# Two pixels instead of four in a row of the corner table of a deformable convolution

## The chip, the cores and the metric

The kernel runs on one core of one Trainium2 chip, in fp32. The metric is the device time of one execution in microseconds (us); the runs shown are three executions of the kernel before.

## The reference

The input x has four images of 128 channels and 64 x 64 pixels. Two layers are applied to it.

Layer 0 normalizes x in groups of channels and adds a deformable 3 x 3 convolution of the result. An ordinary convolution gives, for every pixel and each of the nine taps, an offset (dy, dx) and a mask. The tap samples the normalized image at a fractional position by bilinear interpolation between four corners; what is outside the image counts as zero. The 9 x 128 samples of a pixel, times their masks, are multiplied by the convolution's weight.

```
y0, x0 = floor(py), floor(px);  wy, wx = py - y0, px - x0
v = v00*(1-wy)*(1-wx) + v01*(1-wy)*wx + v10*wy*(1-wx) + v11*wy*wx
out = einsum('bckhw,ock->bohw', v * mask, weight) + bias
```

Layer 1 sees the 4096 pixels of an image as 4096 tokens of 128 numbers, normalizes them, and applies attention and a feed-forward net:

```
qkv = ring products of cos(heads + theta)      # 16 heads of 8 numbers; q = k = v
ctx = softmax(q q^T / sqrt(8)) q               # over all 4096 tokens of the image
x1  = LN(x + ctx W);  out = LN(x1 + FFN(x1))
```

A mixture of eight experts, of which each token takes the best two, follows with another normalization and a residual. The output has the shape of x.

## The kernel before, in words

**Stages.** Each image is a batch b. `prepare(b)` does layer 0 and makes the keys, queries and values: `group_norm`, `corner_table`, `offsets`, then `deform`, which runs over 8 chunks of 512 pixels and starts `convolved` and `features` for each chunk. The attention of batch b runs over head groups (4 groups of 4 heads), chunks of 512 queries and 32 blocks of 128 keys. A step computes the scores of one block (`scores`, TensorE at L1143, the exponential on ScalarE at L1152) and adds their product with the values (`context`, L1160). For most pairs of neighbouring query chunks, exponentials computed once are transposed, written to DRAM (`etd`, L1045), fetched again (`et`, L1079) and used at L1099. `finish` does the rest of layer 1 for a chunk.

**Order.** The program of TensorE, VectorE, SyncE and GpSimd is written out in one order by a planner, `Beside`. It holds estimates of durations and puts pieces of `prepare`, `finish` and others between the attention steps: each piece says by `need(...)` what it costs on TensorE and VectorE, and `beside.later(...)` puts off a DMA until what it sends should be ready. Nothing of that changes at run time. SyncE (SP) issues nearly all DMAs in this order: what stands behind a DMA in its queue waits until that one has been issued, and one that waits for data holds up all that follow. ScalarE (ACT) issues the constants' loads at the start, and then some table writes. GpSimd (POOL) issues the gathers.

Batch 0 has nothing to run beside it: it is prepared alone until its first chunk is done, and then the first head group's attention takes keys as they come. `prepare(b + 1)` runs beside the attention of batch b.

**The table.** The image with a border is 67 x 67 = 4489 positions (`TW` = 67). In DRAM each position has a row of `4 * C` = 512 numbers (2 KB): the pixels at its four corners. There are two tables, used by even and odd batches. A gather (L573) fetches 128 rows, one for each of 128 output pixels, for one tap:

```
nc.gpsimd.indirect_dma_start(
    out=v[:, k, :], out_offset=None, in_=tab,
    in_offset=bass.IndirectOffsetOnAxis(ap=idx[:, j, kk : kk + 1], axis=0),
)
```

VectorE multiplies three such fetches by the twelve weights `wt` (L587), adds the four corners in two steps (L589, L590) and transposes the sums (L597).

**Filling the table.** `borders` writes zeros to two rows and two columns on each side: two DMAs of 67 columns x 2 rows (L303) and two of 63 rows x 2 columns (L304) a table. For table 0 they stand near the head of ACT's queue, ahead of `wom_sb` (L310, the weights of the offsets), `bom_sb` (L314) and the other constants. For table 1 they stand in SP's queue at the start of `prepare(1)`, just behind the four loads of the image (L764). The tile framework makes each pixel write wait for the borders of its table, and each gather for all writes before it.

`corner_table` takes four chunks of 1024 pixels. A chunk is normalized (L454), transposed on TensorE (L462), copied to a tile `tok` (L465, three buffers, which `deform` uses too) and written to the table (L474). A pixel is a corner of four positions, so `put` writes each chunk four times (k = 0 to 3), for odd and even image rows apart (`par`): 8 DMAs of 256 KB a chunk, 32 a batch, each in pieces of 512 bytes. In batch 0 ACT issues the odd k.

`offsets` computes in two halves: the convolution on TensorE (L505), a bias on VectorE (L512), a transpose (L517, L520), then on VectorE the floor, the index `idx` (L549) and the weights `wt` (L557), with an exponential for the mask on ACT (L527).

Of the kernel before, what the change touches and what calls it, by code (L numbers as in the profile page):

```python
# [9 lines left out]
F32 = mybir.dt.float32  # L10
# [3 lines left out]
ALU = mybir.AluOpType  # L14
# [9 lines left out]
C = 128  # L24
HH = 64
WW = 64
# [11 lines left out]
TW = WW + 3  # L38
# [157 lines left out]
def need(pe=0.0, dve=0.0, lat=0.0, hold=False, after=0.0):  # L196

    return pe, dve, lat, hold, after  # L200


def ve(n, ops=1):

    return ops * (0.17 + n / 960.0)
# [6 lines left out]
def tr(n):  # L212

    return 0.13 + 0.115 * n
# [3 lines left out]
def kernel(  # L218
# [22 lines left out]
    nc = tc.nc  # L241
# [7 lines left out]
    dram = ctx.enter_context(tc.tile_pool(name="table", bufs=1, space=DRAM))  # L249
# [14 lines left out]
    def misc(name):  # L264
        if alone:
            return ps_s.tile([P, 2, 512], F32, tag="sc", name=name)[:, 0, :]
        return ps_m.tile([P, 512], F32, tag="misc", name=name)
# [25 lines left out]


    NTAB = 2
    tabs = [dram.tile([TW * TW, 4 * C], F32, name=f"tab{i}") for i in range(NTAB)]
    def borders(tab, queue):
        zero = work.tile([P, 4, 4, P], F32, tag="st", name="zero", bufs=NST)
        zero = zero.rearrange("p r h x -> p r (h x)")[:TW, :2]
        nc.gpsimd.memset(zero, 0.0)  # L300
        tv = tab.rearrange("(y x) c -> y x c", x=TW)
        for s in (0, TW - 2):
            queue.dma_start(out=tv[s : s + 2].rearrange("y x c -> x y c"), in_=zero)  # L303
            queue.dma_start(out=tv[2 : TW - 2, s : s + 2, :], in_=zero[: TW - 4])  # L304

    borders(tabs[0], nc.scalar)

    wom_sb = cpool.tile([P, KK, 32], F32, name="wom_sb")
# [87 lines left out]
    for i in range(NFX):  # L396
        t = big.tile([P, 4, QR], F32, name=f"fx{i}")
        nc.gpsimd.memset(t, 0.0)
        h = t[:, :, : HEADS * QW].rearrange("p j (h d) -> p j h d", d=QW)
# [47 lines left out]
    def corner_table(b, xc, mg, rs, tab):  # L447


        tv = tab.rearrange("(y x) (k c) -> y x k c", x=TW, c=C)  # L450
        for ch in range(NBLK // 8):
            yield need(dve=ve(1024), lat=0.3)
            part = xc[:, 1024 * ch : 1024 * (ch + 1)]
            nc.vector.tensor_scalar(part, part, mg, rs, ALU.subtract, ALU.mult)  # L454
            tok = work.tile([P, 3, 4 * C], F32, tag="v", name=f"tok{b}_{ch}", bufs=NV)
            tok = tok.rearrange("p k (q c) -> p (k q) c", c=C)[:, :8]
            for i in range(0, 8, 4):
                yield need(pe=tr(4), dve=ve(512), lat=FREE)
                pt = misc(f"tok_ps{b}_{ch}_{i}")
                for n in range(4):  # L460
                    j = 8 * ch + i + n
                    nc.tensor.transpose(  # L462
                        pt[:, C * n : C * (n + 1)], xc[:, P * j : P * (j + 1)], ident
                    )
                nc.vector.tensor_copy(  # L465
                    tok[:, i : i + 4, :], pt.rearrange("p (i c) -> p i c", c=C)
                )
            def put(ch=ch, tok=tok):
                for par in range(2):
                    for k in range(4):  # L470
                        y0 = 16 * ch + par + 2 - k // 2
                        x0 = 2 - k % 2
                        queue = nc.scalar if b == 0 and k % 2 else nc.sync
                        queue.dma_start(  # L474
                            out=tv[y0 : y0 + 15 : 2, x0 : x0 + WW, k].rearrange("y x c -> x y c"),
                            in_=tok[WW * par : WW * (par + 1)],
                        )

            beside.later(beside.dve, put)

    def offsets(b, xn, idx, wt):

        xn3 = xn.rearrange("p (h w) -> p h w", w=WW)
        HB = NBLK // 2
        for half in range(2):
            blk = slice(HB * half, HB * (half + 1))

            def temp(name, n):
                return work.tile([P, HB, n], F32, tag="p2", name=f"{name}{b}_{half}", bufs=NP2)

            for n, k in enumerate((4, 0, 1, 2, 3, 5, 6, 7, 8)):
                for top in range(0, 8, 4):
                    last = n == KK - 1 and top == 4
                    yield need(pe=MM256, dve=ve(512) if last else 0.0, lat=0.2 if last else FREE, hold=not last)
                    if n == 0 and top == 0:
                        po = misc(f"om_ps{b}_{half}")
                        p3 = po.rearrange("p (h w) -> p h w", w=WW)
                    dy, dx = k // 3 - 1, k % 3 - 1  # L500
                    for c in range(4):
                        r0 = 32 * half + 8 * c
                        ra, rb_ = max(r0 + top, -dy), min(r0 + top + 4, HH - dy)
                        ca, cb = max(0, -dx), min(WW, WW - dx)
                        nc.tensor.matmul(  # L505
                            p3[32 * c : 32 * (c + 1), ra - r0 : rb_ - r0, ca:cb],
                            lhsT=wom_sb[:, k, :],
                            rhs=xn3[:, ra + dy : rb_ + dy, ca + dx : cb + dx],
                            start=(n == 0 and top == 0), stop=last,
                        )  # L510
            oc = work.tile([P, 512], F32, tag="p2", name=f"oc{b}_{half}", bufs=NP2)
            nc.vector.tensor_scalar(oc, po, bom_sb, None, ALU.add)  # L512
            yield need(pe=tr(4), dve=ve(432), lat=0.2)
            om = temp("om", 27)
            pt = misc(f"oc_ps{b}_{half}")
            for i in range(4):
                nc.tensor.transpose(  # L517
                    pt[:, P * i : P * (i + 1)], oc[:, P * i : P * (i + 1)], ident
                )
            nc.vector.tensor_copy(  # L520
                om.rearrange("p (c i) k -> p i c k", i=4),
                pt.rearrange("p (i c k) -> p i c k", c=4, k=32)[:, :, :, :27],
            )

            yield need(dve=ve(288, 2))
            mk = temp("mk", KK)
            nc.scalar.activation(mk, om[:, :, 18:27], AF.Exp, scale=-1.0)  # L527
            p = om[:, :, 0:18]
            nc.vector.tensor_tensor(p, p, grid_sb[:, blk, :], ALU.add)
            nc.vector.tensor_scalar(p, p, LO, HI, ALU.max, ALU.min)  # L530
            yield need(dve=ve(288, 3))
            fl, up, ix = temp("fl", 18), temp("up", 18), temp("ix", KK)
            nc.vector.tensor_scalar(fl, p, ROUND, None, ALU.add)
            nc.vector.tensor_scalar(fl, fl, ROUND, None, ALU.subtract)
            nc.vector.tensor_tensor(up, fl, p, ALU.is_gt)
            yield need(dve=ve(288, 2))
            nc.vector.tensor_tensor(fl, fl, up, ALU.subtract)
            nc.vector.tensor_tensor(p, p, fl, ALU.subtract)
            yield need(dve=ve(144, 3) + 0.6)

            def of_axis(t, a):
                return t.rearrange("p j (k a) -> p j k a", a=2)[:, :, :, a]

            nc.vector.tensor_scalar(mk, mk, 1.0, None, ALU.add)
            nc.vector.reciprocal(mk, mk)
            nc.vector.tensor_scalar(
                ix, of_axis(fl, 0), float(TW), 2.0 * TW + 2.0, ALU.mult, ALU.add
            )
            nc.vector.tensor_tensor(idx[:, blk, :], ix, of_axis(fl, 1), ALU.add)  # L549
            yield need(dve=ve(288))  # L550

            nc.vector.tensor_scalar(up, p, -1.0, 1.0, ALU.mult, ALU.add)
            for dy in range(2):
                yield need(dve=ve(144, 3), lat=0.2)
                nc.vector.tensor_tensor(ix, of_axis(p if dy else up, 0), mk, ALU.mult)
                for dx in range(2):
                    nc.vector.tensor_tensor(  # L557
                        wt[:, blk, :, 2 * dy + dx], ix, of_axis(p if dx else up, 1), ALU.mult
                    )

    def deform(b, tab, idx, wt):
# [677 lines left out]
    with tc.manual_schedule(engines={PE, DVE, SP, POOL}):  # L1239
# [6 lines left out]
        while n < len(steps):  # L1246
# [11 lines left out]
            b, g, sc, ts, kind = runs[run]  # L1258
# [26 lines left out]
            if following:  # L1285
# [5 lines left out]
                if following[:2] != (b, g):  # L1291
                    for c in range(NCH):
# [5 lines left out]
                        k = (*following[:2], c)  # L1298
# [99 lines left out]
```

## Time and profile before

| | |
|---|---|
| three executions | 8044.03, 8049.18, 8049.44 us; median 8049.18 |
| the profiled execution | 7885.99 us, span 7884.2 us |
| TensorE (PE) busy | 7082.8 us, 90% of the span |
| ScalarE (ACT) busy | 6818.3 us, 86% |
| VectorE (DVE) busy | 4542.1 us, 58% |
| GpSimd (POOL) busy | 1615.5 us, 20% |
| mean granted TensorE clock | 0.948 |
| DMA | 1779.27 MB, mean 226 GB/s; written to HBM 697.34 MB |
| table writes | 128 DMAs of 256 KB; borders 8 of 252 or 268 KB |
| gathers | 1152, 302.06 MB |

The profile is of one execution on the chip. Its rows by slice (`PE`, `ACT`) give the busy share in 40 equal slices in tenths, 9 being 90% or more. A line of a group gives source line, engine, operation, what is written from what, and the number of instructions; behind the bars, busy time and mean duration, then the idle time of the engine before them and what ended it. SPq, ACTq and POOLq are an engine's queue, where its DMAs are issued. A matmul's busy time is not its peak.

### The profile page before, as it was taken

The page shows a single profiled execution, that of the slowest core. Times are in us where ns is not written, and L with a number is a line of the kernel's source. Part 1 is how long each engine was busy: PE and PEld are TensorE (multiplying, and loading weights), DVE is VectorE, ACT ScalarE, POOL GpSimd, SP SyncE. Part 2 cuts the span into 40 slices and gives each one's busy share as a digit, 9 for nine tenths or more (in the row PEclk, how much of TensorE's full clock was granted, in tenths as well). Part 3 has the DMA queues.
Part 4 walks back from the last instruction along what each step waited for, and adds up shares of the span by engine and source line. Part 5 has one row for each costly group of instructions (what it writes and reads, how often), then busy time and mean ns, then how long its engine had stood idle before and what let it go on. Part 6 is the DMA issues. An engine that isn't in the chain of part 4 may idle for free.

```text
span 7884.2 us, 182857 instructions
## 1 busy us (share of the span) xinstructions
PE 7082.8 (90%) x74144; PEld 2507.9 (32%) x74144; DVE 4542.1 (58%) x9062; ACT 6818.3 (86%) x7393; POOL 1615.5 (20%) x1326
## 2 busy tenths in 40 slices
PE   2257799998999999999999999989999999999997
PEld 1112223322333333333333333333333333333332
DVE  5766267665245577676554477777444554545433
ACT  0146798888999999998999998989999999999996
POOL 4545044332000233232000133333000000000000
PEclk6678899999999999999999999999999999999998
DMA  6766479888566888888765789898765578787762
GB/s 182 206 189 198 132 209 314 282 277 259 169 181 176 243 274 284 257 256 268 203 189 165 228 281 280 279 311 275 216 187 165 147 237 247 239 251 231 246 212 81
DMA packets 968730, 1779.27 MB, mean 226 GB/s; under 512 B 170896, under 2 KB 434072, under 8 KB 914124
## 3 DMA queue, kind: packets, MB, share of 16 engines
q1 hardware_dynamic: 862878, 1457.84, 61.4%
q0 software_dynamic: 92160, 302.06, 12.2%
q8 instruction: 581, 9.52, 0.5%
q10 hardware_dynamic: 12846, 7.67, 0.4%
q14 instruction: 265, 2.17, 0.1%
HBM read 1069.86 MB, written 697.34 MB: 224 GB/s over the span
## 4 chain that ended last, share of the span: by engine, by line
PE 76%; DMA 9%; DVE 5%; issue 4%; SPq 3%; ACT 2%; POOL 2%; ACTq 0%; POOLq 0%; DVEq 0%
PE acc L1160 37%; PE sc L1143 22%; PE acc L1099 6%; PE e_ps L272 3%; PE conv_ps L272 3%; DMA et<-etd 2%; ACT e L1152 2%; PE f_ps L272 2%; DMA kT<-kTd 1%; POOL v L573 1%; DMA sT<-smd 1%; DMA v<-tab,idx 1%; DVE v L587 1%; DMA qT<-qTd 1%; PE om_ps L505 1%
## 5 line engine op out<-in xcount | busy, mean ns | idle before, releaser
L1152 ACT ACTIVATE e<-sc 128x1024 f32<-128x1024 f32 x7352 | 6814.8, 1079 | 902.6 <-PE sc L1143 732.0
L1160 PE MATMUL acc<-e,qf 128*32 128x512 f32 x29408 | 3929.8, 607 | 11.9 <-DVE part L1315 7.0
L1143 PE MATMUL sc<-qT,kT 32*128 32x512 f32 x14704 | 2332.9, 501 | 318.2 <-ACT e L1152 118.8
L1143 PEld LDWEIGHTS sc<-qT,kT 32*128 32x128 f32 x14704 | 935.6, 184 | 3660.4 <-ACT e L1152 3231.6
L573 POOL DMA_INDIRECT v<-tab,idx x1152 | 1425.4, 1237 | 1646.4 <-DVE tr L597 1002.1
L1035 DVE STREAM_TRANSPOSE st<-e 128x1024 f32<-128x1024 f32 x840 | 993.9, 1222 | 996.7 <-ACT e L1152 875.1
L1160 PEld LDWEIGHTS acc<-e,qf 128*32 128x32 f32 x29408 | 796.3, 110 | 555.8 <-issue 321.9
L374 POOL TENSOR_TENSOR r<-ln_t,expo 128x4 f32<-128x4 f32 x96 | 106.5, 1109 | 3332.8 <-DVE ln_t L372 3304.8
L587 DVE TENSOR_TENSOR v<-v,wt 128x1536 f32<-128x1536 f32 x384 | 666.7, 1736 | 108.4 <-DMA v<-tab,idx 93.0
L1099 PE MATMUL acc<-et,qf 128*32 128x128 f32 x13440 | 548.9, 282 | 83.2 <-DMA et<-etd 83.2
L272 PE MATMUL conv_ps<-sT,wconv_sb 128*32 128x256 f32 x4608 | 375.3, 406 | 164.3 <-DMA sT<-smd 164.2
L968 DVE TENSOR_TENSOR eo<-e_ps,gt 128x512 f32<-128x512 f32 x256 | 174.9, 684 | 444.7 <-PE e_ps L272 444.3
L1099 PEld LDWEIGHTS acc<-et,qf 128*32 128x32 f32 x13440 | 319.7, 110 | 291.6 <-issue 189.6
L589 DVE TENSOR_TENSOR v<-v 128x768 f32<-128x768 f32 x384 | 368.8, 960 | 11.0
L597 DVE STREAM_TRANSPOSE tr<-v 128x128 f32<-128x128 f32 x1152 | 266.9, 283 | 54.5 <-DMA etd<-st 44.1
L1321 DVE COPY cu<-acc 128x512 f32<-128x512 f32 x121 | 83.7, 692 | 351.1 <-PE acc L1160 351.1
L590 DVE TENSOR_TENSOR v<-v 128x384 f32<-128x384 f32 x384 | 215.2, 560 | 13.3
L272 PEld LDWEIGHTS conv_ps<-sT,wconv_sb 128*32 128x32 f32 x4608 | 102.5, 111 | 320.8 <-issue 295.4
L272 PE MATMUL f_ps<-w_sb,h 128*32 128x128 f32 x4096 | 166.7, 283 | 0.0
L374 POOL TENSOR_TENSOR rstd<-lt_t,expo 128x4 f32<-128x4 f32 x32 | 47.8, 1495 | 553.7 <-DVE lt_t L372 532.6
L853 DVE TENSOR_SCALAR h<-h_ps,b_sb 128x512 f32<-128x512 f32 x128 | 94.6, 741 | 91.0 <-PE h_ps L851 75.5
L729 POOL COPY fx<-rn 128x512 f32<-128x512 f32 x32 | 30.1, 941 | 550.7 <-DVE rn L728 352.8
(221 smaller groups left out, 3006.3 us busy)
## 6 DMA issues: line engine op xcount, KB each, us to landing
etd<-st SPq DMA_DIRECT2D x1680, 256.0 KB
et<-etd SPq DMA_DIRECT2D x420, 1024.0 KB
kT<-kTd SPq DMA_DIRECT2D x384, 256.0 KB
smd<-tr SPq DMA_DIRECT2D x384, 192.0 KB
sT<-smd SPq DMA_DIRECT2D x384, 192.0 KB
qf<-fqd SPq DMA_DIRECT2D x384, 144.0 KB
qT<-qTd SPq DMA_DIRECT2D x156, 256.0 KB
atd<-cu SPq DMA_DIRECT2D x128, 256.0 KB
```

The lines of the kernel that those rows point to most:

```text
L272: nc.tensor.matmul(dst[c : c + 32], lhsT=lhsT[:, c : c + 32], rhs=rhs, start=start, stop=stop)
L573: nc.gpsimd.indirect_dma_start(out=v[:, k, :], out_offset=None, in_=tab, in_offset=bass.IndirectOffsetOnAxis(ap=idx[:, j, kk : kk + 1], ax ...
L587: nc.vector.tensor_tensor(v4, v4, w12[:, :, None].to_broadcast([P, 12, C]), ALU.mult)
L589: nc.vector.tensor_tensor(v[:, :, : 2 * C], v[:, :, : 2 * C], v[:, :, 2 * C :], ALU.add)
L590: nc.vector.tensor_tensor(v[:, :, :C], v[:, :, :C], v[:, :, C : 2 * C], ALU.add)
L597: nc.vector.transpose(out=tr9[:, k, :, j % 4, :], in_=v[:, k, :C].rearrange("p (c i) -> p c i", i=32),)
L968: nc.vector.tensor_tensor(ws[hf], pe.rearrange("p (e c) -> p e c", c=C), gt[:, i, 4 * hf : 4 * (hf + 1), None].to_broadcast([P, 4, C]), AL ...
L1035: nc.vector.transpose(out=st[:, :, 2 * pr : 2 * pr + 2, :].rearrange("p o h (q j) -> p o (h q) j", j=32), in_=es[pr].rearrange("p h (q o i ...
L1099: nc.tensor.matmul(acc[32 * h : 32 * (h + 1), P * kt : P * (kt + 1)], lhsT=qf[:, t, QW * h : QW * h + 32], rhs=e[:, :, h, 32 * t : 32 * (t ...
L1143: nc.tensor.matmul(ps[i // 2][:, i % 2, :], lhsT=kT[h : h + 32, P * (t % 4) : P * (t % 4 + 1)], rhs=qT[h : h + 32, :], start=True, stop=True,)
L1152: nc.scalar.activation(e, ps[pr], AF.Exp, scale=1.0 / math.sqrt(HD))
L1160: nc.tensor.matmul(acc[32 * h : 32 * (h + 1), :], lhsT=qf[:, t % 4, QW * h : QW * h + 32], rhs=es[h // 2][:, h % 2, :], start=(t == ts[0]) ...
```

## The change

A row of the table holds two pixels, the position's own and the one below, 256 numbers (1 KB). A gather still takes 512 numbers from the start of a row, and so reads the row and the next one, which is the position to the right. One row is added at the end of the table for the last position's neighbour, with a zero write of its own in `borders`. The pixel writes are done for k = 0 and 1 alone: 4 DMAs of 256 KB a chunk. In batch 0 ACT issues the writes of odd image rows of the first three chunks (6 DMAs), SP the other 10. The fetched corners come in another order (down before right), so `wt` is filled in that order.

```diff
-    tabs = [dram.tile([TW * TW, 4 * C], F32, name=f"tab{i}") for i in range(NTAB)]
+    tabs = [dram.tile([TW * TW + 1, 2 * C], F32, name=f"tab{i}") for i in range(NTAB)]
     def borders(tab, queue):
         zero = work.tile([P, 4, 4, P], F32, tag="st", name="zero", bufs=NST)
-        zero = zero.rearrange("p r h x -> p r (h x)")[:TW, :2]
+        zero = zero.rearrange("p r h x -> p r (h x)")[:TW, :2, : 2 * C]
         nc.gpsimd.memset(zero, 0.0)
-        tv = tab.rearrange("(y x) c -> y x c", x=TW)
+        tv = tab[: TW * TW].rearrange("(y x) c -> y x c", x=TW)
+        queue.dma_start(out=tab[TW * TW :], in_=zero[:1, 0])
         for s in (0, TW - 2):
             queue.dma_start(out=tv[s : s + 2].rearrange("y x c -> x y c"), in_=zero)
             queue.dma_start(out=tv[2 : TW - 2, s : s + 2, :], in_=zero[: TW - 4])
...
     def corner_table(b, xc, mg, rs, tab):
-        tv = tab.rearrange("(y x) (k c) -> y x k c", x=TW, c=C)
+        tv = tab[: TW * TW].rearrange("(y x) (k c) -> y x k c", x=TW, c=C)
...
             def put(ch=ch, tok=tok):
                 for par in range(2):
-                    for k in range(4):
-                        y0 = 16 * ch + par + 2 - k // 2
-                        x0 = 2 - k % 2
-                        queue = nc.scalar if b == 0 and k % 2 else nc.sync
+                    for k in range(2):
+                        y0 = 16 * ch + par + 2 - k
+                        queue = nc.scalar if b == 0 and par == 1 and ch < 3 else nc.sync
                         queue.dma_start(
-                            out=tv[y0 : y0 + 15 : 2, x0 : x0 + WW, k].rearrange("y x c -> x y c"),
+                            out=tv[y0 : y0 + 15 : 2, 2 : 2 + WW, k].rearrange("y x c -> x y c"),
                             in_=tok[WW * par : WW * (par + 1)],
                         )
...
                     nc.vector.tensor_tensor(
-                        wt[:, blk, :, 2 * dy + dx], ix, of_axis(p if dx else up, 1), ALU.mult
+                        wt[:, blk, :, 2 * dx + dy], ix, of_axis(p if dx else up, 1), ALU.mult
                     )
```

## The prediction

> **What bounds the kernel now.** I read the page first, then the timeline and the stretches around the places where the table is built, then the waits there. The page says that over most of the span TensorE and ScalarE are full, so a DMA saved there is worth little; the change can pay only where both stand still.
>
> ```profile
> span 7884.2 us, 182857 instructions
> ...
> PE   2257799998999999999999999989999999999997
> ...
> ACT  0146798888999999998999998989999999999996
> ...
> q1 hardware_dynamic: 862878, 1457.84, 61.4%
> ...
> L573 POOL DMA_INDIRECT v<-tab,idx x1152 | 1425.4, 1237 | 1646.4 <-DVE tr L597 1002.1
> ```
>
> PE and ACT reach 9 tenths only after some eight slices of 197 us: the first 870 us are batch 0, whose deformable convolution has little attention to run beside it. All that delays its first gather delays the rest. The timeline of the first 85 us shows what does:
>
> ```profile
> 2.37 9.78 ACTq L304 DMA_DIRECT2D tab<-zero  x1
> ...
> 12.18 0.63 ACTq L303 DMA_DIRECT2D tab<-zero  x1
> 12.85 9.00 ACTq L304 DMA_DIRECT2D tab<-zero  x1
> ...
> 34.42 34.51 SPq L474 DMA_DIRECT2D tab<-tok  x16
> ...
> 48.30 28.57 ACTq L474 DMA_DIRECT2D tab<-tok  x16
> ...
> 61.08 1.29 DVE L465 COPY tok<-tok_ps 128x512 f32<-128x512 f32 x2 [34.10 <-DMA tab<-tok]
> 62.29 0.74 DVE L512 TENSOR_SCALAR oc<-om_ps,bom_sb 128x512 f32<-128x512 f32 x1
> ...
> 81.03 1.25 POOL L573 DMA_INDIRECT v<-tab,idx  x1 [65.38 <-DVE ix L555]
> ```
>
> Columns: start, duration, engine, line, operation, and in brackets the idle time before and what ended it. The zero borders hold up ACT's queue twice. The pixel writes wait for them until 34.42, though the first tok was ready at 19.3 (the copy of 18.57 and its 0.69). The fourth tok reuses the first one's buffer, so VectorE stands 34.10 us until the first chunk's eight writes have landed; the offsets (L512) are behind it. The exponential on ACT then waits for the last of ACT's own writes, at 76.87. So the first gather is at 81.03.
>
> The same borders come again for table 1, on SP:
>
> ```profile
> 877.55 8.68 SPq L304 DMA_DIRECT2D tab<-zero  x1
> 886.27 0.60 SPq L303 DMA_DIRECT2D tab<-zero  x1
> 886.92 11.14 SPq L304 DMA_DIRECT2D tab<-zero  x1
> 898.15 1.71 SPq L1132 DMA_DIRECT2D qT<-qTd  x3
> ...
> 908.55 1.22 PE L1143 MATMUL sc<-qT,kT 32*128 32x512 f32 x6 [37.14 <-DMA qT<-qTd]
> ```
>
> The stretches of the same place show the cause; a row has the window, its length, the busy time of PE, PEld, DVE, ACT and POOL, the clock, the DMA share and GB/s:
>
> ```profile
> 890.00:895.00 5.00, 0.00 (x0) 0.00 (x0) 0.00 (x0) 0.00 (x0) 0.00 (x0) 0.50 0.07 26
> ```
>
> Nothing computes, and 0.07 is one DMA engine of 16. TensorE waits 37.14 us for a query tile queued behind the borders.
>
> In batches 1 to 3 the table is written beside full attention. Only short holes there come from it:
>
> ```profile
> 977.62 1.94 ACT L1152 ACTIVATE e<-sc 128x1024 f32<-128x1024 f32 x2 [5.14 <-PE sc L1143]
> ...
> 2557.46 1.08 PE L1099 MATMUL acc<-et,qf 128*32 128x128 f32 x16 [3.26 <-DMA et<-etd]
> ...
> 4384.40 0.65 PE L1099 MATMUL acc<-et,qf 128*32 128x128 f32 x16 [1.87 <-DMA et<-etd]
> ```
>
> **What the Trainium skill says.** DMA: Bandwidth & Descriptors, "Why a DMA increments its semaphore by 16 and not by 1": a hardware DMA is split over the largest count up to 16 that divides the slowest dimension of both sides, and takes the lowest-numbered engines. 67 columns give one engine, 63 rows nine. The trace agrees (0.07 above). Same page, "Queues, rings and completion order": each DMA engine takes a ring's descriptors in order, so a transfer's share on that one engine stands behind the borders; the query tiles that land only at 908.5 agree. Same page, "Issuing engines are not separate DMA queues": ACT's and SP's writes share the 16 engines, so moving writes between the queues by itself buys only issue time. From 34 to 76 the trace has 221 to 237 GB/s with both queues writing.
>
> **The change part by part.**
>
> *Borders.* Each is one extra 1 KB DMA, and the other four carry half the bytes in as many or twice as many packets. Packet records of the trace: 2048 bytes take 84 ns, 512 bytes 27, 1152 bytes 51, 4096 bytes 159 (medians). So about 8 ns plus 0.037 ns a byte, and 46 ns for 1024 bytes. The one engine carries 2x134 packets of 2048 bytes and 2x7 of 4096: 22.5+2.2 = 24.7 us. Head: its 2048s start at 7.3 and it ends at 32.9, which fits. After: 268 packets of 1 KB and 28 more: 296x46 = 13.6 us. Saving 11.1 us each time. If packets were paid by count alone it would be nothing, by bytes alone 12.4; I take 11, keep 8 to 13. The extra DMA is some 0.5 us of issue, inside this.
>
> *Head of batch 0.* Borders are done near 21, SP writes from about 22.5 (34.42-11, with 0.5 for the rest). ACT's constants, held up behind the borders until 32.2, start near 21 and took 15.5 us to 47.7, so ACT's first table writes come near 37, and there are 6 where there were 16. Chunk 0's writes land near 41 (two on SP long done, two on ACT, each some 1.3 to 2 us to issue and some 2 more). Volume agrees: 4.2 MB of table and 1.9 MB of constants at 235 GB/s take 26 us from 22.5, so 48.5 for all. The fourth tok's copies: 41 to 42.5. TensorE's first half of the offsets has finished by then: it waits for wom (then near 23) and its own transposes (29.1) and takes 9.55, so 38.7. L512 at 42.5. From L512 to the gather there are 8.3 us of VectorE work once ACT's wait is gone (62.29 to the last L538 at 67.85 is 5.6, then 78.56 to 81.03 is 2.5, and handover): first gather at 51, table complete at about 50. That is 30 us earlier. What is late next is the second half of the offsets: TensorE's 9.9 us, hidden before beneath the wait for ACT, now start only after the transposes at 44.5 and end at 54.4; L512 of that half moves from 82.47 to 54.7, 27.8 us. I take 27, bounds 11 (only the borders' part) and 32. No fixed time lies behind it: batch 0's chain follows from its gathers.
>
> *Borders of table 1.* The engine starts on them at 907.4-24.7 = 882.7, after the inputs of L764. It ends 11 us earlier, and the query tile lands at 897.5. Saving 11, kept 8 to 13. SP's queue behind it (three query loads) moves with it.
>
> *Table writes of batches 1 to 3.* 16 of 32 DMAs of 256 KB go. SP saves 16 issues of about 1.3 us, 21 us a batch, and the engines 8192 packets of 36 ns over 16, 18 us. Only the stalls count: 2.6 us of PE around 977 (the key tile sits in SP's queue behind the writes until 971.3), 3.6 near 2557 (PE busy 16.36 of 20), 3.0 near 4384 and 4415 (18.13 and 18.83 of 20). Together 9.2; SP keeps half the writes, so I take 8, bounds 2 and 13. The rest lies beside ACT's exponentials, which are full there (19.9 of 20), and costs or brings nothing; were that cover gone, it would be worth up to 18 us a batch.
>
> *The gather.* Still 1152 of 128 fetches of 2 KB, now starting at multiples of 1 KB. The built program keeps the fetch at 512 elements and halves only the index factor. At nothing: POOL's 956 ns and the packets stay. *Weights*: the same VectorE operations in another place of each four, nothing. The instruction order on PE, DVE and POOL is the same in both programs.
>
> Sum: 27+11+8 = 46 us off the profiled 7886.0 (span 7884.2 and 1.8 around it), to 7840. The median of the timed runs, 8049.2, is 163 us or 2.1% above that execution; waits on DMAs should weigh the same there, so 8049-46 = 8003.
>
> **Rivals.** *The head gives only the borders' 11 us.* For it: ACT's constants are issued ahead of its table writes, and the fourth tok still waits for two of them. Against: 10 fewer ACT writes and half the volume. Then 11+11+8 = 30, 8019.
>
> *The gather is cut at the new row.* The fetch is twice the declared row. Software builds a descriptor pair for each operation (the Trainium skill, DMA: Bandwidth & Descriptors, "SWDGE vs HWDGE vs iDMA"; no run here shows a price by count). If each fetch became two, a gather would take up to 0.95 us more on POOL. In batch 0, with 288 gathers and POOL 14.5% of the chain of the first 600 us (87 us), that is 87 to 275 us; later batches hide it, POOL being idle four fifths of the time. Net 41 to 229 slower, say 8150. It decides from 46/288 = 0.16 us a gather if all is on the chain, from half a gather's time if only those 87 us are. Against it: the built program's 512 elements.
>
> *All hidden.* A granted clock that falls as the holes go, or batch 0 paced elsewhere: 8049. Against it: idle time at the head and at 875 to 908 on all four computing engines.
>
> *More.* The holes of batches 1 to 3 also cost clock afterwards (0.76 to 0.83 from 910 to 930), and the head reaches its bound: 46+16 = 62, 7987.
>
> **How the numbers follow.** Chances: main case 0.62 (7990 to 8012 by its bounds), head only the borders 0.20, more 0.06, hidden 0.05, gather cut 0.07. Faster 0.88, same 0.05, slower 0.07, where 0.2% (16 us) is about what a measurement here can tell from no change. The range from 7985 to 8030 takes in the first three and their unknown costs, and leaves out the last two and tails.
>
> **What would show it.** Right: first gather near 51 (wrong above 65), no 34 us wait at L465; the hole before the first query matmul after the borders about 26 us instead of 37; 1 KB packets near 46 ns; L573 still near 956 ns (median) with 64 packets of 4 KB each. A gather of 1.2 us or more, or a borders' hole still over 33 us, makes the prediction wrong.

## The result and the profile after

The kernel after takes 8011.48 us in the median of five runs (7999.12 to 8018.62), the kernel before 8049.44 (8044.03 to 8062.78): a ratio of 0.9947, 95% interval 0.9932 to 0.9961, 38 us less. In a second comparison the medians are 7971.94 and 8019.53, a ratio of 0.9937 (0.9924 to 0.9951), 48 us less. The prediction said 46 less and 8003.

The page after, with the same rows as the page before in the prediction (span, busy share of TensorE and ScalarE in 40 slices, the queue's packets, MB and share of the DMA engines, the gathers):

```profile
span 8010.8 us, 182782 instructions
...
PE   2257898989999999998999999989999999999997
...
ACT  0146798878999988897999989888999999999996
...
q1 hardware_dynamic: 834494, 1443.15, 60.1%
...
L573 POOL DMA_INDIRECT v<-tab,idx x1152 | 1414.4, 1228 | 1741.1 <-DVE tr L597 1129.1
```

The span is longer than the 7884.2 shown of before, though the kernel is faster. The first profile of before is of an execution 2% shorter than all its timed runs; the profile after agrees with its own. So traces are compared below with a second profile of before (before_again), taken on one chip with a second of after (after_again). The gathers cost what they did: 1228 ns in the mean, 1224 in before_again.

The head, from the timeline of the profile after:

```profile
2.50 6.73 ACTq L305 DMA_DIRECT2D tab<-zero  x1
...
10.41 6.20 ACTq L305 DMA_DIRECT2D tab<-zero  x1
...
25.79 23.02 SPq L474 DMA_DIRECT2D tab<-tok  x10
...
36.24 7.91 ACTq L474 DMA_DIRECT2D tab<-tok  x6
42.22 1.29 DVE L466 COPY tok<-tok_ps 128x512 f32<-128x512 f32 x2 [13.49 <-DMA tab<-tok]
43.42 0.74 DVE L512 TENSOR_SCALAR oc<-om_ps,bom_sb 128x512 f32<-128x512 f32 x1
...
52.69 1.24 POOL L573 DMA_INDIRECT v<-tab,idx  x1 [35.30 <-DVE ix L555]
```

The borders' column DMAs (now L305) block ACT for 6.7 and 6.2 us instead of 9.8 and 9.0. The fourth tok (now L466) still waits for the first chunk's writes, of which ACT's two come last, 13.49 us instead of 34.10. The first gather is 28 us earlier.

The hole behind the borders of table 1, that is the stretch in which TensorE waits for the first query tile queued behind them, same view:

```profile
862.81 6.31 SPq L305 DMA_DIRECT2D tab<-zero  x1
869.16 0.64 SPq L304 DMA_DIRECT2D tab<-zero  x1
869.85 5.62 SPq L305 DMA_DIRECT2D tab<-zero  x1
875.57 1.37 SPq L1132 DMA_DIRECT2D qT<-qTd  x3
...
882.06 1.22 PE L1143 MATMUL sc<-qT,kT 32*128 32x512 f32 x6 [25.16 <-DMA qT<-qTd]
```

TensorE stands 25.16 us where it stood 37.14.

### The profile page after: what moved, and what is told of

Read it like the earlier page. It is cut to its first block, busy times and chain, and to the rows that moved or that the text cites. A ratio compares the mean times of both kernels' runs of the same rounds, so it can differ in the third digit from the quotient of the medians.

```text
span 8010.8 us, 182782 instructions
## 1 busy us (share of the span) xinstructions
PE 7199.2 (90%) x74144; PEld 2539.6 (32%) x74144; DVE 4541.2 (57%) x9062; ACT 6829.4 (85%) x7393; POOL 1603.5 (20%) x1326
## 3 DMA queue, kind: packets, MB, share of 16 engines
q0 software_dynamic: 92160, 302.06, 11.9%
## 4 chain that ended last, share of the span: by engine, by line
PE 78%; DMA 7%; issue 4%; DVE 4%; ACT 3%; SPq 2%; POOL 1%; another core or an unknown queue 1%; ACTq 0%; POOLq 0%; DVEq 0%
PE acc L1160 38%; PE sc L1143 23%; PE acc L1099 6%; PE e_ps L272 3%; ACT e L1152 3%; PE conv_ps L272 3%; PE f_ps L272 2%; DMA et<-etd 2%; DMA kT<-kTd 1%; POOL v L573 1%; DMA sT<-smd 1%; DMA v<-tab,idx 1%; DVE v L587 1%; PE om_ps L505 1%
## 5 line engine op out<-in xcount | busy, mean ns | idle before, releaser
L1160 PE MATMUL acc<-e,qf 128*32 128x512 f32 x29408 | 3976.4, 609 | 23.5 <-issue 8.4
L1143 PE MATMUL sc<-qT,kT 32*128 32x512 f32 x14704 | 2387.7, 502 | 389.7 <-ACT e L1152 169.8
L1143 PEld LDWEIGHTS sc<-qT,kT 32*128 32x128 f32 x14704 | 955.3, 184 | 3772.4 <-ACT e L1152 3073.3
L573 POOL DMA_INDIRECT v<-tab,idx x1152 | 1414.4, 1228 | 1741.1 <-DVE tr L597 1129.1
L587 DVE TENSOR_TENSOR v<-v,wt 128x1536 f32<-128x1536 f32 x384 | 666.0, 1734 | 97.6 <-DMA v<-tab,idx 73.7
```

The costliest lines, as they stand in the source:

```text
L573: nc.gpsimd.indirect_dma_start(out=v[:, k, :], out_offset=None, in_=tab, in_offset=bass.IndirectOffsetOnAxis(ap=idx[:, j, kk : kk + 1], ax ...
L587: nc.vector.tensor_tensor(v4, v4, w12[:, :, None].to_broadcast([P, 12, C]), ALU.mult)
L1143: nc.tensor.matmul(ps[i // 2][:, i % 2, :], lhsT=kT[h : h + 32, P * (t % 4) : P * (t % 4 + 1)], rhs=qT[h : h + 32, :], start=True, stop=True,)
L1160: nc.tensor.matmul(acc[32 * h : 32 * (h + 1), :], lhsT=qf[:, t % 4, QW * h : QW * h + 32], rhs=es[h // 2][:, h % 2, :], start=(t == ts[0]) ...
```

## The experiments

All ratios are to the kernel before, run on the same chip. The theory is the prediction's: one DMA engine's border work at two places, the pixel writes at the head, and the short holes beside attention.

**before_again** and **after_again** are the two kernels unchanged.

> The kernel before, once more, for a profile on the same chip as the other runs. The first profile of before took 7886 us where its timed runs took 8049; the profile of the kernel after took 8012.5, as its timed runs. Against each other these two profiles show after 15 to 25 us ahead up to 1100 us, and then 150 us behind, lost while the gathers of batches 1 to 3 run. Theory A (the first profile of before is of an execution that differs from its timed runs, the change has no part in the 150 us): this profile is near 8050 us and stays 15 to 50 us behind after's in every batch. Theory B (the change makes the gathers of batches 1 to 3 slower, by 100 us or more, and gains as much elsewhere): this profile is near 8050 us but is 100 us or more ahead of after's at the end of batch 3's gathers.

> The kernel after, beside the others. By the sum of the prediction 46 us under before (0.9943); by the first measurement 38 (0.9947). A rival, that the head gives only the borders' 11 us and the borders of table 1 another 11: 22 to 30 us under before (0.9965).

before_again's profiled run took 8017.1 us, within its timed runs (8013.51 to 8034.70), and it stays behind after's second profile by 24.5 us at attention step 240 of 7352 exponentials, 37.3 at 480, 39.8 at 1920 and 65.5 at the end (that profile is the fastest of after's five runs, 7951.62). It is behind the first profile of after too, by 20.5 us at step 240 and by 3.0 at the end. The first profile of before is 131 us ahead of the second, with the same program. So theory B is out: before_again ends ahead of neither profile of after, and the 150 us between the first two profiles are no part of the change. Theory A's 15 to 50 us do not hold throughout, though: two single profiles do not give the change in the total, which is read from the timed runs. after_again came at 0.9937. From the list of waits (total us, times, longest), before_again:

```profile
PE sc L1143 <- DMA qT<-qTd: 113.2, 8, 37.3
...
PE acc L1099 <- DMA et<-etd: 54.4, 14, 11.1
```

after_again:

```profile
PE sc L1143 <- DMA qT<-qTd: 99.3, 8, 26.1
...
PE acc L1099 <- DMA et<-etd: 24.0, 7, 9.7
```

The 37.3 is the hole; in after_again it is 25.62 (at 877.3), and the 26.1 of the list is another wait, near 212, that both have. Of the 30 us by which the second line falls, only the waits of before_again near 2613, 4474 and 4510 (4.23, 1.48 and 2.09 us) lie at table writes of batches 2 and 3; the rest is not shown to come from the change.

The gather's rival, a fetch cut in two, is out by these traces: 92160 packets of the gathers' queue in both, 4 KB packets of 206 and 205 ns (mean), a gather 954 and 953 ns (median).

**borders16** spreads the borders. (All diffs from here are shortened; `...` marks what is left out.)

```diff
-        zero = zero.rearrange("p r h x -> p r (h x)")[:TW, :2, : 2 * C]
+        zero = zero.rearrange("p r h x -> p (r h x)")[:, : 4 * C]
...
+        tv = tab[: TW * TW].rearrange("(y x) c -> y (x c)", x=TW)
...
+        n = 2 * TW * 2 * C // P
         for s in (0, TW - 2):
-            queue.dma_start(out=tv[s : s + 2].rearrange("y x c -> x y c"), in_=zero)
-            queue.dma_start(out=tv[2 : TW - 2, s : s + 2, :], in_=zero[: TW - 4])
+            rows = tab[s * TW : (s + 2) * TW].rearrange("a c -> (a c)")
+            queue.dma_start(out=rows.rearrange("(p f) -> p f", p=P), in_=zero[:, :n])
+            for y0, y1 in ((2, 50), (50, TW - 2)):
+                queue.dma_start(
+                    out=tv[y0:y1, 2 * C * s : 2 * C * (s + 2)], in_=zero[: y1 - y0]
+                )
```

> After, with the borders written by DMAs whose slowest dimension is 128, 48 or 15 instead of 67 or 63; the same zeros. If the stall at the borders is one DMA engine's work, 296 packets of 46 ns, as the prediction has it: the wait of the first score matmul behind the borders of table 1 falls from about 26 us by 12 to 13, and the head gains 2 to 5 us (the pixel writes start at 21 instead of 25.8, TensorE's offsets at 30.7 bound the rest); 15 to 18 us under after. Rival, that the stall is the size of the borders on all engines or a wait of SP for the writes before: nothing changes, within 5 us of after.

It took 7961.13 us, 0.9925 (0.9911 to 0.9938), 11 us under after in the medians. Its timeline:

```profile
36.48 1.29 DVE L471 COPY tok<-tok_ps 128x512 f32<-128x512 f32 x2 [8.49 <-DMA tab<-tok]
...
47.30 1.19 POOL L578 DMA_INDIRECT v<-tab,idx  x1 [30.64 <-DVE ix L560]
...
853.68 1.22 PE L1148 MATMUL sc<-qT,kT 32*128 32x512 f32 x6 [15.57 <-DMA qT<-qTd]
```

In the hole the DMA engines stood mostly idle in after_again and are nearly full here. From the table by stretch (as in the prediction; the last two columns are the DMA share and GB/s), after_again and then borders16:

```profile
867.00:872.00 5.00, 0.00 (x0) 0.00 (x0) 0.00 (x0) 0.00 (x0) 0.00 (x0) 0.50 0.16 48
...
846.00:850.00 4.00, 0.00 (x0) 0.00 (x0) 0.00 (x0) 0.00 (x0) 0.00 (x0) 0.50 0.99 335
```

The same zeros on more engines: the hole falls by 10 us from after_again's 25.62 (12 to 13 were expected), the first gather comes 6 us earlier than its 53.26 (2 to 5 were expected). That the stall came from the borders' work being left to few engines is shown; the two steps sum to 16, within the expected 15 to 18, while the medians gained 11, with intervals that overlap.

**borders_twice** puts the load of the one engine back.

```diff
+        dv = dups[tabs.index(tab)][: TW * TW].rearrange("(y x) c -> y x c", x=TW)
         for s in (0, TW - 2):
-            queue.dma_start(out=tv[s : s + 2].rearrange("y x c -> x y c"), in_=zero)
-            queue.dma_start(out=tv[2 : TW - 2, s : s + 2, :], in_=zero[: TW - 4])
+            for v in (tv, dv):
+                queue.dma_start(out=v[s : s + 2].rearrange("y x c -> x y c"), in_=zero)
+                queue.dma_start(out=v[2 : TW - 2, s : s + 2, :], in_=zero[: TW - 4])
```

`dups` are scratch tables in DRAM that nothing reads.

> After, with the four border DMAs done a second time to a scratch table that nothing reads, on the same queues: the bytes of before's borders, in twice the packets. One DMA engine then carries 2 x 296 packets of 46 ns, 27 us, instead of 13.6. If a border set costs what its one engine needs: the wait behind the borders of table 1 goes from 25.6 to 38 to 40 us, the first gather moves from 53 to 62 to 67, and the time is 22 to 27 us over after. Rival, that the head's gain came from the pixel writes alone and hides the borders there: 11 to 14 us over after, first gather below 57.

0.9972 (0.9962 to 0.9982): with after at 0.9937 to 0.9947, 20 to 28 us over it by the ratios, with intervals that do not overlap. Its timeline:

```profile
66.62 1.19 POOL L576 DMA_INDIRECT v<-tab,idx  x1 [49.17 <-DVE wt L560]
...
899.66 1.22 PE L1146 MATMUL sc<-qT,kT 32*128 32x512 f32 x6 [38.31 <-DMA qT<-qTd]
```

The first gather is back by 13 us, the hole by 12.7, for 13.6 us of packets each, so the rival of 11 to 14 us, with the first gather below 57, is out. The number of DMAs does not set the hole: before's 37.31 us came from the same bytes in four DMAs, this one from nine.

**writes_twice** puts the pixel writes back, **writes_late** those of batches 1 to 3 alone.

```diff
-                    for k in range(2):
+                    for kk in range(4):
+                        k = kk // 2
                         y0 = 16 * ch + par + 2 - k
-                        queue = nc.scalar if b == 0 and par == 1 and ch < 3 else nc.sync
+                        queue = nc.scalar if b == 0 and kk % 2 else nc.sync
                         queue.dma_start(
-                            out=tv[...
+                            out=(dv if kk % 2 else tv)[...
```

`dv` is again a scratch table. In writes_late kk takes 0 and 2 only where b is 0, and the queue is chosen as in after.

> After, with each pixel write of the table done a second time to a scratch table that nothing reads: 32 DMAs of 256 KB a batch again, queues as in before (in batch 0 ACT issues 16). The borders stay half. By the prediction the first gather goes back to about 70 (before's 81 less the borders' 11), 16 to 18 us later than after's, and the short holes of batches 1 to 3 come back, 8 us: 24 to 26 us over after. Rival, that the halved borders are all of the gain (moved along the whole head): within 5 us of after. Rival, that traffic beside attention costs more than its visible holes (18 us of engine time a batch): 50 to 70 us over after.

> After, with the pixel writes done twice as in writes_twice, but in batches 1 to 3 only. Batch 0 and both borders stay as in after. From the profiles the scalar engine's idle time in the 100 us around the table writes of batches 2 and 3 should go back from 0.4 and 0.5 us to 4 to 5 each, and near 0 to 3 us in batch 1: 8 to 14 us over after (the prediction's term was 8, with bounds 2 and 13). The rival, that what traffic costs beside attention is its engine time: 45 to 60 us over after.

writes_twice: 0.9966 (0.9956 to 0.9977), 22 us over after in the medians of the same chip, with intervals that do not overlap. writes_late: 0.9955 (0.9938 to 0.9971), 6 to 14 us over after by the ratios (8 to 14 were expected; 45 to 60, the rival, is out), but its interval overlaps those of after. writes_twice's head:

```profile
25.63 29.99 SPq L477 DMA_DIRECT2D tab<-tok  x16
36.32 28.91 ACTq L477 DMA_DIRECT2D dup<-tok  x16
...
48.24 1.29 DVE L468 COPY tok<-tok_ps 128x512 f32<-128x512 f32 x2 [19.92 <-DMA tab<-tok]
...
65.26 1.28 ACT L530 ACT_TABLE_LOAD   x1 [65.26 <-DMA dup<-tok]
68.97 1.19 POOL L576 DMA_INDIRECT v<-tab,idx  x1 [51.99 <-DMA dup<-tok]
```

ACT ends its 16 writes at 65.2, and the exponential with the gather behind it follows: 68.97 against after_again's 53.26, 15.7 us for the writes at the head, beside the borders' 13. The fourth tok waits only 6 us longer; the other three fifths of the loss are ACT's own queue ahead of its exponential. With 32 writes ACT issues 16, as before the change; 32 writes with only six on ACT were not run, so how much of the head's gain is the halved count and how much ACT's shorter queue is not shown.

For batches 1 to 3 the traces give the scalar engine's idle time (us) from 10 us before a batch's first pixel write to 90 after:

| | batch 1 | batch 2 | batch 3 | sum |
|---|---|---|---|---|
| before | 17.7 | 6.2 | 3.5 | 27.4 |
| before_again | 19.4 | 7.8 | 5.5 | 32.7 |
| after | 18.0 | 0.4 | 0.4 | 18.8 |
| after_again | 18.2 | 0.4 | 0.4 | 19.0 |
| writes_twice | 18.2 | 4.7 | 3.9 | 26.8 |
| writes_late | 19.7 | 6.1 | 1.1 | 26.9 |

**sp_only** changes the queue alone.

```diff
-                        queue = nc.scalar if b == 0 and par == 1 and ch < 3 else nc.sync
+                        queue = nc.sync
```

> After, with all 16 pixel writes of batch 0 on SP, none on ACT. The fourth tok then waits for SP's own early writes and not for ACT's, which come only when the constants have been issued: its wait of 13.6 us falls to 5 to 7, the offsets' first half on TensorE (done near 39) bounds L512, and the first gather is at 49 to 51 instead of 53. Rival, that 16 writes on one queue are late themselves: the gather waits for the table and comes at 53 to 58.

Its timeline:

```profile
25.58 22.31 SPq L474 DMA_DIRECT2D tab<-tok  x16
...
36.84 1.29 DVE L466 COPY tok<-tok_ps 128x512 f32<-128x512 f32 x2 [7.96 <-DMA w<-in_w_dram]
40.35 0.75 DVE L512 TENSOR_SCALAR oc<-om_ps,bom_sb 128x512 f32<-128x512 f32 x1 [2.22 <-PE om_ps L505]
...
52.46 1.25 POOL L573 DMA_INDIRECT v<-tab,idx  x1 [34.91 <-DVE om L529]
```

The wait at the fourth tok falls to 7.96 and L512 comes at 40.35, bounded by TensorE as expected. The gather does not follow: it comes at 52.46, 12 us after L512 where after_again has 10. I expected 49 to 51. The profile names VectorE as the releaser, but the index that the gather needs is ready at 47.13, while the DMA engines are busy with the table until 51 and idle then (timeline, and two stretches):

```profile
46.82 0.31 DVE L549 TENSOR_TENSOR idx<-ix,fl 128x144 int32<-128x144 f32 x1
...
47.20:51.00 3.80, 2.92 (x52) 1.96 (x44) 2.94 (x8) 0.00 (x0) 0.00 (x0) 1.00 0.81 190
51.00:52.40 1.40, 0.18 (x2) 0.00 (x0) 1.12 (x3) 0.33 (x1) 0.00 (x0) 1.00 0.00 0
```

By the packet records the last 512-byte packet of SP's queue, which the table writes are made of, ends at 50.94, 1.5 us before the gather. In after the same times are 51.19 and 52.69 (index ready at 50.64), in after_again 51.76 and 53.26 (50.34), in borders16 45.98 and 47.30 (45.58): the gather follows that packet by 1.3 to 1.5 us, and the index by 1.7 to 5.3. So the first gather waits for the last of the table, in after too. The rival had the wait right, though its 53 to 58 came too late. The one run (7994.7 us, 0.993 of before's median) can't be told from after.

**best** joins borders16 and sp_only and moves the borders of table 1.

```diff
+    borders(tabs[1], nc.scalar)
     is_lo = cpool.tile([32, 1], F32, name="is_lo")
...
-        if b == 1:
-            borders(tab, nc.sync)
```

> borders16 with batch 0's pixel writes all on SP, and the borders of table 1 issued on ACT's queue right after the constants, at some 35 us, instead of on SP at the start of batch 1's preparation. The wait of the score matmul near 850 us falls from 15.6 to 8 to 10 (SP spent 6.7 us on the borders there); the head stays within 3 us of borders16. 5 to 9 us under borders16, 15 to 25 under after. Rival, that the rest of that wait is the image loads and key writes alone: within 2 us of borders16.

7995.07 us, 0.9923 (0.9904 to 0.9942). Its timeline:

```profile
859.76 1.22 PE L1147 MATMUL sc<-qT,kT 32*128 32x512 f32 x6 [12.16 <-DMA qT<-qTd]
```

The hole is 12.16, not 8 to 10; the first gather (49.86) is 2.6 us behind borders16's, within the 3 allowed; the ratio is that of borders16, where 5 to 9 us less were expected, as the rival had it. In what is left of the hole the DMA engines are full: their share is 0.99 from 848 to 852 us and 1.00 from 852 to 856, while the query loads, issued from 851.30 on, land just before 859.76. The key and image transfers issued ahead of them are the likely load; this was not tested. Both borders16 and best beat before; their ratios are below after's, with intervals that overlap, and which of the two is faster can't be told.

## Why the prediction was right

**Borders.** 1 KB packets have a median of 46 ns in the trace after, as worked out. The Trainium skill's rule (DMA: Bandwidth & Descriptors, "Why a DMA increments its semaphore by 16 and not by 1") carried the step, and the traces agree: the same zeros with slowest dimensions of 128, 48 and 15 instead of 67 and 63 cut the hole from 25.6 to 15.6 us. 11 us a set were predicted; the hole fell by 12.0 between the first profiles (37.14 to 25.16) and by 11.7 between the second (37.31 to 25.62). In the other three runs with after's borders it is 23.82 to 24.66.

**Head.** Predicted 51 for the first gather, measured 52.69 and 53.26. SP's writes began at 25.8 instead of 22.5, which the fourth tok did not show: it waited for ACT's writes, begun at 36.2 as reckoned (37). The last wait was not the one that was reckoned with: the chain from L512 was to end at 51 and the table to be complete at 50, but the index was ready first and the table's last packets (51.19, 51.76) released the gather. The two were meant to be a microsecond apart, so the number held. The second half of the offsets was named as late next: predicted at 54.7, it came at 59.98 and 55.32. TensorE had finished it at 55.65 in the slower case, and VectorE stood idle up to it with a releaser that the profile does not resolve:

```profile
45.26 10.39 PE L505 MATMUL om_ps<-xc,wom_sb 128*32 128x256 f32 x144
...
59.98 0.75 DVE L512 TENSOR_SCALAR oc<-om_ps,bom_sb 128x512 f32<-128x512 f32 x1 [6.97 <-remote]
```

The first product of weights and samples (L587) moved from 97.57 to 74.31 between the first profiles and from 97.38 to 69.61 between the second, 23.3 and 27.8 us for 27. The rival that left the head 11 us is ruled out by writes_twice.

**Batches 1 to 3.** 8 us were predicted, with bounds 2 and 13. By the table above the scalar engine's idle time fell by 8.6 us between the first profiles and by 13.7 between the second; with the writes put back it rose by 7.8 (writes_twice) and 7.9 (writes_late). The sum was about right, in part by luck, for its parts were not: batch 1 was to give 2.6 and gave -0.3 and 1.2, while batches 2 and 3 together gave 8.9 and 12.5, where TensorE's holes were counted as 6.6 and something was taken off for the half that SP keeps. There the exponentials stood longer than TensorE (6.2 us for TensorE's 3.6 in batch 2 of the first profile), and the writes that SP keeps left no hole. The timed runs alone do not show this term, as writes_late's interval overlaps after's.

**Gather and weights** at nothing: confirmed by the traces; VectorE is busy for 4541.9 us in before_again and 4542.1 in after_again. By terms then 12, 28 and 9 to 14 make 49 to 54 by the traces for 46 predicted, and 38 and 48 timed. Of the 28 at the gather, 24.5 are left at step 240 in the second profiles and 15 between the first two, and of the 15.7 that writes_twice loses there 10.7; so the prediction's sentence that no fixed time lies behind the head held only in part, and where the rest goes isn't settled. One slip in the working: the main case's 7990 to 8012 takes the head at no less than 27 us; with its stated bound of 11 it would reach 8028.

## What to carry to other kernels

Small DMAs whose slowest dimension has no large divisor up to 16 (here 67) can hold up a whole core: look for a hole in which the DMA share is near one sixteenth (0.07 here), and reshape the transfer as well as shrinking it. Halving traffic pays where a queue stands in front of something awaited, here a buffer's release and an exponential behind ACT's own DMA issues (15.7 us at the head), and much less beside engines that are busy anyway (8 to 14 us of idle time for three batches). Where the profile names a releaser that had long been done, look at the packets: the wait may be for a DMA. Before traces are subtracted, compare each profile's own time with its timed runs.

## What the runs showed of the hardware beyond that

Two executions of one program differed by 131 us in their profiles (7886 and 8017). Counted by the exponentials of attention, the difference stays at 36 to 37 us from step 1400 to 2000, at 90 from 3200 to 3800 and at 129 to 132 from 5000 on, where few gathers run or none; it grows between these, beside the 288 gathers of a batch each time. There TensorE's weight loads for the scores idle with no releaser that the profile shows. First profile of before, list of waits:

```profile
PEld sc L1143 <- issue: 368.6, 224, 38.0
```

before_again:

```profile
PEld sc L1143 <- issue: 644.0, 590, 38.2
```

DMA packets (4 KB packets of the gathers 206 ns in both, mean) and the mean clock (0.948 and 0.950) hardly differ. The cause was not tried and stays open.

Packet times by size on the hardware queues, medians of the traces: 27 ns for 512 bytes, 46 for 1 KB, 84 for 2 KB, 159 for 4 KB, 309 for 8 KB.
